# Four graph-attention layers on one core: layer 0's norms computed during layer 3, and layer 3's first head in whole chunks

## The chip, the cores and the metric

The kernel runs on one core of a Trainium2 chip. A core has a matrix engine (TensorE, PE in the profile, with its weight loads shown as PEld), a vector engine (VectorE, DVE), an activation engine (ScalarE, ACT), a general one (GpSimd, POOL) and a queue engine (SyncE, SP), with SBUF as working memory, PSUM as the memory that PE writes its products to, and DMA queues between SBUF and HBM. The metric is the device time of one execution in microseconds (us); lower is better. The kernel before takes 2933.27 us, the median of 3 runs (2932.54 to 2933.40).

## What is computed

16 graphs ("batches") of 1024 nodes with 256 features go through four layers of graph attention. The input x is 16x1024x256 in float32, and adj, of 0 and 1, is 16x1024x1024. Every layer begins with a norm and adds its attention to x:

```python
h = jnp.maximum(_layernorm(x, axis=-1), 0.0)
x = x + _Ll_gnn_ref(h, adj, W, a)          # l = 0, 1, 2, 3
```

Layer 0 shows the pattern. A weight between node i and node j is a function of one number per row plus one number per column, masked by adj, and the weights sum the projected nodes:

```python
Wh = jnp.einsum('bnf,fo->bno', h, W)
f1 = Wh @ a1
f2 = Wh @ a2
e = jax.nn.leaky_relu(f1[:, :, None] + f2[:, None, :], negative_slope=SLOPE)
e = jnp.where(adj == 0, NEG_INF, e)
attention = jax.nn.softmax(e, axis=-1)
h_prime = jnp.einsum('bij,bjo->bio', attention, Wh)
```

Layers 1 and 2 have other functions of the sum, and an elu over the result. Layer 3 has four heads of 64 features; each has its own projection and weights, and its result goes through a relu, gets h added, and is normed over the 64 features.

## The kernel before, in words

**Layout.** A batch's 1024 nodes are NI = 8 blocks of P = 128 nodes on the partitions; `x_b` holds x as 128 x 8 x 256. Blocks are normed and projected in four pairs.

**A layer's start.** `project` (L315) takes a pair: DVE subtracts the mean and cuts at zero (`centered`, L302, or L325 for batch 0), PE turns the blocks (L338), ACT copies them to `hT` (L340), PE multiplies by W (L345) into an accumulator in PSUM, and `evict` takes it to `V` (L413 to L417) with a scale `rstd`, the inverse root of the squared deviations. For this `center_by_sums` (L299) lets ACT square the block with its mean as bias and sum it (L309), and POOL raises two columns to the power of minus a half (L292, L293). The sums for the means come with the previous layer's last operation, but in layer 0 nothing is before, so DVE sums x (L517). Batch 0 takes its statistics from another instruction (L323).

**Attention.** Exponentials of sums are products, so a weight is a maximum or minimum over a row of numbers and a column, times the mask. `weigh` (L354) lets PE spread one number per node over a `row` in PSUM (one buffer of 128 x 1024; L374, or L574 for layer 3's heads after the first), and DVE makes eight blocks of weights from it (L367), with eight buffers for each of two streams. `attend` (L445) multiplies the blocks with V on PE (L461), one block of result at a time, and projects finished pairs for the next layer in between.

**Layer 3.** Each head has two accumulators: `acc`, for values (`add_values`, L596), and `total`, for the sums of weights (`add_totals`, L606); both are filled by 32-column products through `in_tiles` (L581, L586). Four blocks of weights are a chunk, two chunks a head. Heads 1 to 3 do totals and values of a chunk together, and have the row of the next head (R in the change's name) placed ahead of the first chunk. Head 0 does the values of both chunks, then head 1's row is made from `thirds_T` (L640, L645), and then come the totals of both chunks. After each head ACT copies the two accumulators (L663), and after each copy comes a step of `testing` (a sum over one block of adj, L175) and one of `coming` (loads of the batch after next); PE turns the copies (L670, L678), DVE divides (L681), and `center` (L538) and `rescale` (L558) norm the head on DVE, ACT and POOL.

**Order.** Two streams, of even and odd batches, are generators that yield estimated times; at L719 to L727 the stream that is behind by these estimates goes on. A scheduler then settles each engine's order from that program order; operations handed to `keep_in_program_order` keep theirs, and products under `high_priority` go first. Each accumulator name has two PSUM buffers for each stream. `load` (L128) is the generator `coming`: it narrows adj through a DRAM buffer by POOL's DMA queue, turns it into `mask` by four DMA transposes on SP's queue (L155), and fetches x (L124), one step at a time; `x_b` and `mask` have three buffers, `ex`, the exponentials of layer 3, two.

Of the kernel before, what the change touches and what calls it, by code (L numbers as in the profile page):

```python
# [32 lines left out]
F32 = mybir.dt.float32  # L33
BF = mybir.dt.bfloat16
# [7 lines left out]
P = 128  # L42
# [19 lines left out]
def short_path(ctx: ExitStack, tc: tile.TileContext, ins: dict, out: bass.AP, bad: bass.AP):  # L62
# [65 lines left out]
    def load(b: int):  # L128


        narrow = narrows[b % 2]
        rows = narrow.bitcast(U8)
        if b == 0:

            for h in range(NH):
                for t in range(2):
                    cast = nc.gpsimd.dma_start(
                        halves[h].bitcast(U8).rearrange("(c t q) j -> t c q j", t=2, q=P)[t],
                        adj[b].rearrange("(c q t) j -> t c q j", t=2, q=P)[t, :, :, ts(h, HALF)],
                    )  # L140
                    tc.keep_in_program_order(cast)
        else:
            for c in range(NI // 2):
                cast = nc.gpsimd.dma_start(
                    rows.rearrange("(c t q) j -> c q t j", t=2, q=P)[c],
                    adj[b, ts(c, 2 * P), :].rearrange("(q t) j -> q t j", t=2),
                )
                tc.keep_in_program_order(cast)
        if b < 2:
            fetch_nodes(b)  # L150
        yield

        mask = masks[b] = nodes.tile([P, NI // 2, N, 2], U8, name="mask")
        for c in range(NI // 2):
            turn = nc.sync.dma_start_transpose(  # L155
                mask[:, c].rearrange("p n t -> p (n t)").bitcast(BF),
                halves[c // NH][:, ts(c % NH, P)] if b == 0 else narrow[:, ts(c, P)],
            )
            tc.keep_in_program_order(turn)
            yield  # L160
        if b > 1:
            fetch_nodes(b)
            yield

    def test(b: int):
# [130 lines left out]
    def accumulator(b: int) -> bass.AP:  # L296
        return psum.tile([P, HALF], F32, name=f"acc{b % 2}")

    def center_by_sums(xb: bass.AP, minus_mean: bass.AP, pair: int, centered: bass.AP) -> bass.AP:  # L299

        for n in range(2):
            nc.vector.tensor_scalar(  # L302
                centered[:, n, :], xb[:, 2 * pair + n, :], minus_mean[:, n : n + 1], 0.0,
                op0=ALU.add, op1=ALU.max,
            )
        squared = small.tile([P, 2], F32, name="squared")
        for n in range(2):
            square = work.tile([P, D], BF, name="square", bufs=1)
            nc.scalar.activation(  # L309
                square, xb[:, 2 * pair + n, :], AF.Square, bias=minus_mean[:, n : n + 1],  # L310
                accum_out=squared[:, n : n + 1],
            )
        return inverse_root(squared, 2, D, LN_EPS)

    def project(b: int, l: int, xb: bass.AP, sums: bass.AP, pair: int, evict):  # L315


        centered = work.tile([P, 2, D], F32, name="centered", bufs=3)
        if sums is None:
            mv = small.tile([P, 2, nc.vector.BN_AGGR_DIM], F32, name="mv", bufs=2)  # L320
            for n in range(2):
                stats = small.tile([P, nc.vector.BN_STATS_DIM], F32, name="stats", bufs=1)
                nc.vector.bn_stats(stats, xb[:, 2 * pair + n, :])  # L323
                nc.vector.bn_aggr(mv[:, n, :], stats)
                nc.vector.tensor_scalar(  # L325
                    centered[:, n, :], xb[:, 2 * pair + n, :], mv[:, n, 0:1], 0.0,
                    op0=ALU.subtract, op1=ALU.max,
                )
            rstd = inverse_root(mv[:, :, 1], 2, D, LN_EPS, D)
        else:  # L330
            minus_mean = small.tile([P, 2], F32, name="minus_mean")
            nc.vector.tensor_scalar_mul(minus_mean, sums[:, ts(pair, 2)], -1.0 / D)  # L332
            rstd = center_by_sums(xb, minus_mean, pair, centered)
        yield 0.5
        turned = psum.tile([P, NK, 2 * P], F32, name="misc")
        for n in range(2):
            for k in range(NK):
                nc.tensor.transpose(turned[:, k, ts(n, P)], centered[:, n, ts(k, P)], ident)  # L338
        hT = wide.tile([P, NK, 2 * P], F32, name="hT", bufs=3)
        nc.scalar.mul(hT, turned, ROOT_D)  # L340
        yield 1.0
        for n in range(2):
            projected = accumulator(b)[:, : D + EXT[l]]
            for k in range(NK):
                nc.tensor.matmul(  # L345
                    projected, hT[:, k, ts(n, P)], W[l][:, k, :],
                    start=(k == 0), stop=(k == NK - 1),
                )
            evict(2 * pair + n, projected, rstd[:, n : n + 1])
        yield 2.5  # L350
# [48 lines left out]
        )  # L399

    def batch(b: int):
        xb = xs.pop(b)
        if b == 0:
            next(preparing)
        coming = load(b + 2) if b + 2 < B else iter(())
# [21 lines left out]
        def begin3():  # L427
            h3 = last["h3"] = single.tile([P, NI, D], F32, name="h3")
            V3 = nodes.tile([P, NI, H, E + 1], F32, name="V", bufs=4)
            ex = last["ex"] = small.tile([P, NI, 3 * H], F32, name="ex", bufs=2)  # L430

            def evict3(i: int, projected: bass.AP, rstd: bass.AP):
                nc.scalar.activation(ex[:, i, :], projected[:, D:], AF.Exp, scale=rstd)
                nc.scalar.mul(h3[:, i, :], projected[:, :D], rstd)
                q = ex[:, i, :H].unsqueeze(2)
                nc.gpsimd.tensor_mul(
                    V3[:, i, :, :E], h3[:, i, :].rearrange("p (h e) -> p h e", h=H),
                    q.to_broadcast([P, H, E]),
                )
                nc.gpsimd.tensor_copy(V3[:, i, :, E:], q)  # L440
                nc.gpsimd.tensor_add(xb[:, i, :], xb[:, i, :], beta)  # L441

            return V3, evict3
# [63 lines left out]
            add_elu(xb[:, i, :], acc, total)  # L507

        V, evict = begin(0)
        sums = small.tile([P, NI], F32, name="sums_of_x")  # L510

        def first(pair: int):
            if b == 0:

                yield from project(b, 0, xb, None, pair, evict)
                return
            nc.vector.tensor_reduce(sums[:, ts(pair, 2)], xb[:, ts(pair, 2), :], AX.X, ALU.add)  # L517
            yield from project(b, 0, xb, sums, pair, evict)

        pairs = [first(pair) for pair in range(NI // 2)]  # L520
        for n in range(NI // 2 + 2):
            for pair in range(max(n - 2, 0), min(n + 1, NI // 2)):
                yield from islice(pairs[pair], 1)
# [82 lines left out]
        def add_totals(h: int, j: int):  # L606
# [4 lines left out]
            ]  # L611
            in_tiles(parts, total, j == 2, j == NI - 4)

        behind = weigh3(0)
        yield from start(behind, b)

# [7 lines left out]
        for h in range(H):  # L624
# [1 line left out]

            acc = accumulator(b)
            total = accumulator(b)
            if h == 0:
                for first in range(0, NI, 4):  # L630
                    for _ in range(4):
                        next(behind)
                    pinned = []
                    for j in (first + 2, first):
                        add_values(h, j)
                    yield 3.6
                for _ in behind:
                    pass
                turned_thirds = psum.tile([3 * QUAD, P], BF, name="misc")
                made = nc.tensor.transpose(  # L640
                    turned_thirds, thirds.rearrange("p t i h -> p (t i h)"), ident_bf
                )
                tc.keep_in_program_order(made)
                thirds_T = small.tile([3 * QUAD, P], BF, name="thirds_T", bufs=1)
                nc.scalar.copy(thirds_T, turned_thirds)  # L645
            behind = weigh3(h + 1)
            yield from start(behind, b)

            for first in range(0, NI, 4):
                pinned = []  # L650
                for j in (first + 2, first):
                    add_totals(h, j)
                    if h > 0:
                        add_values(h, j)
                for _ in range(4):
                    next(behind, None)
                yield 1.8 if h == 0 else 5.4
            for _ in behind:
                pass
            copies = []  # L660
            for accT in (acc, total) if h == 0 else (total, acc):
# [4 lines left out]
            sums, totals = copies if h == 0 else copies[::-1]  # L666
            yield 0.5
            turned = psum.tile([P, NG, P], F32, name="misc")
            for i in range(NG):
# [28 lines left out]
        for _ in coming:  # L698
# [406 lines left out]
```

## Time and profile before

| | |
|---|---|
| time, median of 3 runs | 2933.27 us (2932.54 to 2933.40) |
| the profiled execution's own time | 2933.13 us |
| its span, first to last instruction | 2931.4 us |
| mean granted PE clock | 0.995 |
| one repetition (one batch done) in the middle | 178.5 us, of which PE is busy 174.5, DVE 133.4, ACT 68.2, POOL 61.6 |
| products of layers 0 to 2 (L461) | 6144 records, 1435.6 us of PE |
| products of layer 3 (L586) | 6144 records, 691.7 us of PE |
| weights (L367) | 896, 1102.7 us of DVE |
| ACT's squares for the norms (L309) | 504, 255.7 us and 96.5 us of reading the sums |

A line of the profile's groups gives the source line, the engine, the operation, its result and sources with their sizes, the count, the busy time and the mean duration of one, and the idle time of the engine just before with what ended it. Each float32 product of PE stands as two records. In windows each engine's busy time in a stretch is followed by its count of instructions; a line of the waits says who waited for whom, with the sum, the count and the longest; a line in order of time gives start, duration, engine, line and operation, and in brackets the idle time before.

### The profile page before, as it was taken

Reading aid. Unit: us, or ns where it says so; the run is one execution under the profiler, and the core shown is the slowest. Engines: PE = TensorE matmul, PEld = TensorE weight load, DVE = VectorE, ACT = ScalarE, POOL = GpSimd, SP = SyncE. Lnnn points to the kernel's source line nnn. Section 1 sums busy time; section 2 is a strip of 40 time slices with the busy share of each in tenths; the row PEclk is TensorE's granted clock in tenths of the full one; section 3 lists DMA queues with packets and bytes.
Section 4 is the critical chain, followed back from the end, with each engine's and each line's share of the span. In section 5 each row is a group of like instructions: output and inputs, shape, how many; then the busy total and the mean of one; then the engine's idle time right before and its main releaser. Section 6 shows DMA issues by size and latency. Waiting matters only on the chain.

```text
span 2931.4 us, 44756 instructions
## 1 busy us (share of the span) xinstructions
PE 2810.0 (96%) x16790; PEld 1961.9 (67%) x16790; DVE 2147.9 (73%) x4490; ACT 1088.2 (37%) x3010; POOL 981.3 (33%) x1533
## 2 busy tenths in 40 slices
PE   7999999999999999999999999999999999999986
PEld 5775857668576685766758577685766857667552
DVE  5658688586976859778586885868768587685857
ACT  1333434343343433424334343433434334343332
POOL 2123324243242423424233242432424224242333
PEclk9999999999999999999999999999999999999998
DMA  8204022030321303122031220303203031110101
GB/s 126 39 8 65 30 30 58 8 51 29 37 51 16 56 17 51 37 29 59 1 51 37 30 58 8 51 30 37 51 12 47 29 49 39 15 30 1 22 22 31
DMA packets 127967, 106.14 MB, mean 36 GB/s; under 512 B 79872, under 2 KB 98432, under 8 KB 127744
## 3 DMA queue, kind: packets, MB, share of 16 engines
q0 software_dynamic: 47328, 66.10, 15.4%
q1 hardware_dynamic: 79568, 35.53, 5.4%
q8 instruction: 135, 2.21, 0.3%
q10 hardware_dynamic: 848, 1.57, 0.2%
q14 instruction: 88, 0.72, 0.1%
HBM read 153.49 MB, written 33.55 MB: 64 GB/s over the span
## 4 chain that ended last, share of the span: by engine, by line
PE 59%; DVE 26%; issue 8%; POOL 3%; ACT 3%; DMA 0%; POOLq 0%; ACTq 0%; SPq 0%; DVEq 0%
PE acc L461 36%; DVE weights L367 16%; PE acc L586 10%; PE acc L345 9%; PE misc L338 2%; DVE centered L302 2%; POOL rstd L293 2%; DVE V L417 1%; PE row L374 1%; POOL y L544 1%; DVE y L545 1%; DVE var L555 1%; ACT square L309 1%; DVE y L551 1%; DVE mean L549 1%
## 5 line engine op out<-in xcount | busy, mean ns | idle before, releaser
L461 PE MATMUL acc<-V,weights 128*128 128x257 f32 x6144 | 1435.6, 384 | 33.5 <-DVE weights L367 15.7
L461 PEld LDWEIGHTS acc<-V,weights 128*128 128x128 f32 x6144 | 1136.6, 190 | 281.9 <-DVE weights L367 75.3
L586 PE MATMUL acc<-weights,V 128*32 128x512 f32 x6144 | 691.7, 596 | 12.0 <-DVE weights L367 8.1
L367 DVE SCALAR_TENSOR_TENSOR weights<-row,ex,mask 128x1024 f32<-128x1024 f32 x512 | 629.0, 1272 | 97.3 <-PE row L574 65.8
L345 PE MATMUL acc<-W,hT 128*128 128x259 f32 (+1 forms) x2048 | 516.1, 389 | 38.1 <-ACT hT L340 26.9
L367 DVE SCALAR_TENSOR_TENSOR weights<-row,V,mask 128x1024 f32<-128x1024 f32 x384 | 473.7, 1273 | 0.8 <-PE row L374 0.8
L345 PEld LDWEIGHTS acc<-W,hT 128*128 128x128 f32 x2048 | 378.7, 190 | 135.1 <-ACT hT L340 44.4
L586 PEld LDWEIGHTS acc<-weights,V 128*32 128x32 f32 x6144 | 189.1, 110 | 417.7 <-issue 410.3
L393 ACT ACTIVATE below<-acc,inv 128x256 f32<-128x256 f32 x256 | 121.1, 473 | 813.1 <-DVE inv L386 569.6
L293 POOL TENSOR_TENSOR rstd<-rstd,minus_half 128x2 f32<-128x2 f32 (+1 forms) x321 | 292.8, 912 | 20.3
L309 ACT ACTIVATE square<-x_b,minus_mean 128x256 bf16<-128x256 f32 x504 | 255.7, 507 | 110.3 <-DVE minus_mean L332 105.3
L441 POOL TENSOR_TENSOR x_b<-x_b,beta 128x256 f32<-128x256 f32 x128 | 93.5, 731 | 488.6 <-ACT square L309 483.5
L292 POOL TENSOR_SCALAR rstd<-squared 128x2 f32<-128x2 f32 x252 | 80.0, 317 | 464.0 <-ACT square L309 451.0
L385 DVE TENSOR_SCALAR inv<-acc 128x1 f32<-128x1 f32 x256 | 39.1, 153 | 255.3 <-PE acc L461 254.0
L302 DVE TENSOR_SCALAR centered<-x_b,minus_mean 128x256 f32<-128x256 f32 x504 | 195.7, 416 | 5.1
L340 ACT ACTIVATE hT<-misc 128x512 f32<-128x512 f32 x256 | 150.2, 592 | 129.6 <-PE misc L338 129.3
L396 DVE SCALAR_TENSOR_TENSOR x_b<-below,x_b 128x256 f32<-128x256 f32 x256 | 131.8, 515 | 84.9 <-ACT below L393 83.0
L663 ACT COPY sums<-acc 128x512 f32<-128x512 f32 x128 | 74.9, 585 | 308.6 <-PE acc L586 301.0
L413 ACT ACTIVATE V<-acc,rstd 128x3 f32<-128x3 f32 x384 | 98.4, 261 | 231.1 <-PE acc L345 230.6
L417 DVE TENSOR_SCALAR V<-acc,rstd,V 128x256 f32<-128x256 f32 x256 | 131.4, 537 | 59.8 <-ACT V L413 58.9
L338 PE MATMUL misc<-ident,centered 128*128 128x128 f32 x1024 | 158.7, 277 | 13.7 <-DVE centered L325 11.5
L170 POOL DMA_DIRECT2D adj_i<-in_adj_dram x128 | 74.4, 582 | 290.1 <-ACT adj_i L175 248.8
(96 smaller groups left out, 2212.8 us busy)
## 6 DMA issues: line engine op xcount, KB each, us to landing
adj_i<-in_adj_dram POOLq DMA_DIRECT2D x128, 256.0 KB, 3.9
x_b<-in_x_dram SPq DMA_DIRECT2D x15, 1024.0 KB, 6.4
narrow<-in_adj_dram POOLq DMA_DIRECT2D x60, 256.0 KB, 9.3
out_dram<-y POOLq DMA_DIRECT2D x30, 512.0 KB, 7.5
x_b<-in_x_dram ACTq DMA_DIRECT2D x4, 256.0 KB, 6.1
narrow_half<-in_adj_dram POOLq DMA_DIRECT2D x4, 256.0 KB, 16.9
mask<-narrow SPq DMA_TRANSPOSE x60, 3.7
weights<-in_L_gnn_a_dram SPq DMA_DIRECT2D x3, 256.0 KB, 5.5
```

The costliest lines, as they stand in the source:

```text
L293: nc.gpsimd.tensor_tensor(r, r, minus_half.to_broadcast([P, n]), op=ALU.pow)
L302: nc.vector.tensor_scalar(centered[:, n, :], xb[:, 2 * pair + n, :], minus_mean[:, n : n + 1], 0.0, op0=ALU.add, op1=ALU.max,)
L309: nc.scalar.activation(square, xb[:, 2 * pair + n, :], AF.Square, bias=minus_mean[:, n : n + 1], accum_out=squared[:, n : n + 1],)
L338: nc.tensor.transpose(turned[:, k, ts(n, P)], centered[:, n, ts(k, P)], ident)
L340: nc.scalar.mul(hT, turned, ROOT_D)
L345: nc.tensor.matmul(projected, hT[:, k, ts(n, P)], W[l][:, k, :], start=(k == 0), stop=(k == NK - 1),)
L367: nc.vector.scalar_tensor_tensor(w, r, c(j), masks[b][:, j // 2, :, j % 2], op0=op, op1=ALU.mult)
L393: nc.scalar.activation(below, acc[:, :D], AF.Exp, scale=inv)
L396: nc.vector.scalar_tensor_tensor(xi, below, 1.0, xi, op0=ALU.min, op1=ALU.add)
L417: nc.vector.tensor_scalar(V[:, i, :D], projected[:, :D], rstd, V[:, i, D : D + 1], op0=ALU.mult, op1=ALU.mult,)
L461: nc.tensor.matmul(accs[i], weights[j][:, ts(i, P)], V[:, j, : D + 1], start=(j == 0), stop=(j == NI - 1),)
L586: made = nc.tensor.matmul(accT[ts(n, QUAD), :], values, moving, start=first, stop=last)
```

## The change

1. `norm_ahead` computes the statistics of layer 0 of the batch after next while a batch's layer 3 goes on: ACT sums each block in an Identity pass, POOL makes the negative means, ACT squares and sums, and after the last pair POOL makes all eight `rstd` at once. It has eight steps, two after each head of layer 3 (`next(ahead, None)`). Batch 1's are made in one go at its start; batch 0 keeps its own. `project` takes them as a pair of tiles, so the DVE sums (L517) and the squares in layer 0 go.
2. `load` fetches x ahead of the mask's transposes, and takes its step once before layer 3's heads.
3. Head 0 of layer 3 does totals and values of a chunk together, and the source makes head 1's row, and four of its weights, ahead of head 0's second chunk.
4. `ex` has one buffer.

```diff
-        if b < 2:
-            fetch_nodes(b)
+        if b > 1:
+            yield
+        fetch_nodes(b)
         yield
...
-            yield
-        if b > 1:
-            fetch_nodes(b)
             yield
...
+    def norm_ahead(b: int):
+        totals = small.tile([P, NI], F32, name="totals_of_x", bufs=1)
+        minus_mean = small.tile([P, NI], F32, name="minus_means", bufs=2)
+        squared = small.tile([P, NI], F32, name="squares_of_x", bufs=1)
+        for pair in range(NI // 2):
+            for i in (2 * pair, 2 * pair + 1):
+                square = work.tile([P, D], BF, name="square", bufs=1)
+                tc.keep_in_program_order(
+                    nc.scalar.activation(
+                        square, xs[b][:, i, :], AF.Identity, accum_out=totals[:, i : i + 1]
+                    )
+                )
+            nc.gpsimd.tensor_scalar_mul(
+                minus_mean[:, ts(pair, 2)], totals[:, ts(pair, 2)], -1.0 / D
+            )
+            yield
+            for i in (2 * pair, 2 * pair + 1):
+                square = work.tile([P, D], BF, name="square", bufs=1)
+                tc.keep_in_program_order(
+                    nc.scalar.activation(
+                        square, xs[b][:, i, :], AF.Square, bias=minus_mean[:, i : i + 1],
+                        accum_out=squared[:, i : i + 1],
+                    )
+                )
+            yield
+        rstd = small.tile([P, NI], F32, name="first_rstd", bufs=2)
+        nc.gpsimd.tensor_scalar_add(rstd, squared, D * LN_EPS)
+        nc.gpsimd.tensor_tensor(rstd, rstd, minus_half.to_broadcast([P, NI]), op=ALU.pow)
+        norms_ahead[b] = minus_mean, rstd
...
+        elif isinstance(sums, tuple):
+            minus_mean, rstd = (a[:, ts(pair, 2)] for a in sums)
+            relu_centered(xb, minus_mean, pair, centered)
...
     def batch(b: int):
+        if b == 1:
+            for _ in norm_ahead(b):
+                pass
         xb = xs.pop(b)
+        ahead = norm_ahead(b + 2) if b + 2 < B else iter(())
...
-            nc.vector.tensor_reduce(sums[:, ts(pair, 2)], xb[:, ts(pair, 2), :], AX.X, ALU.add)
-            yield from project(b, 0, xb, sums, pair, evict)
...
+        next(coming, None)
         behind = weigh3(0)
         yield from start(behind, b)
...
-            if h == 0:
-                for first in range(0, NI, 4):
+            if h > 0:
+                behind = weigh3(h + 1)
+                yield from start(behind, b)
+
+            for first in range(0, NI, 4):
+                if h == 0:
                     for _ in range(4):
                         next(behind)
-                    pinned = []
-                    for j in (first + 2, first):
-                        add_values(h, j)
-                    yield 3.6
...
+                if h == 0 and first > 0:
+                    for _ in behind:
+                        pass
...
+                    behind = weigh3(1)
+                    yield from start(behind, b)
+                    for _ in range(4):
+                        next(behind)
                 pinned = []
                 for j in (first + 2, first):
                     add_totals(h, j)
-                    if h > 0:
-                        add_values(h, j)
-                for _ in range(4):
-                    next(behind, None)
-                yield 1.8 if h == 0 else 5.4
+                    add_values(h, j)
+                if h > 0 or first > 0:
+                    for _ in range(4):
+                        next(behind, None)
+                yield 5.4
...
                 next(testing)
                 next(coming, None)
+                next(ahead, None)
```

`relu_centered` is the loop at L301 to L305 as a function of its own.

More of the change, by code (lines that the diff above doesn't have):

```diff
@@ L297, in accumulator, with relu_centered @@
         return psum.tile([P, HALF], F32, name=f"acc{b % 2}")
-    def center_by_sums(xb: bass.AP, minus_mean: bass.AP, pair: int, centered: bass.AP) -> bass.AP:
+    def norm_ahead(b: int):
[27 more added lines that the diff above has]
+        norms_ahead[b] = minus_mean, rstd
+    norms_ahead = {}
+    def relu_centered(xb: bass.AP, minus_mean: bass.AP, pair: int, centered: bass.AP):
         for n in range(2):
@@ L305, in center_by_sums @@
             )
+    def center_by_sums(xb: bass.AP, minus_mean: bass.AP, pair: int, centered: bass.AP) -> bass.AP:
+        relu_centered(xb, minus_mean, pair, centered)
         squared = small.tile([P, 2], F32, name="squared")
@@ L329, in project @@
             rstd = inverse_root(mv[:, :, 1], 2, D, LN_EPS, D)
+        elif isinstance(sums, tuple):
+            minus_mean, rstd = (a[:, ts(pair, 2)] for a in sums)
+            relu_centered(xb, minus_mean, pair, centered)
         else:
@@ L429, in begin3 @@
             V3 = nodes.tile([P, NI, H, E + 1], F32, name="V", bufs=4)
-            ex = last["ex"] = small.tile([P, NI, 3 * H], F32, name="ex", bufs=2)
+            ex = last["ex"] = small.tile([P, NI, 3 * H], F32, name="ex", bufs=1)
             def evict3(i: int, projected: bass.AP, rstd: bass.AP):
@@ L509, in batch @@
         V, evict = begin(0)
[L510 to L516, printed above, removed]
-            nc.vector.tensor_reduce(sums[:, ts(pair, 2)], xb[:, ts(pair, 2), :], AX.X, ALU.add)
-            yield from project(b, 0, xb, sums, pair, evict)
-        pairs = [first(pair) for pair in range(NI // 2)]
+        known = None if b == 0 else norms_ahead.pop(b)
+        pairs = [project(b, 0, xb, known, pair, evict) for pair in range(NI // 2)]
         for n in range(NI // 2 + 2):
@@ L628, in batch @@
             total = accumulator(b)
-            if h == 0:
-                for first in range(0, NI, 4):
+            if h > 0:
[3 more added lines that the diff above has]
+                if h == 0:
                     for _ in range(4):
                         next(behind)
-                    pinned = []
-                    for j in (first + 2, first):
-                        add_values(h, j)
-                    yield 3.6
[L637 to L649, printed above, removed]
+                if h == 0 and first > 0:
+                    for _ in behind:
+                        pass
+                    turned_thirds = psum.tile([3 * QUAD, P], BF, name="misc")
+                    made = nc.tensor.transpose(
+                        turned_thirds, thirds.rearrange("p t i h -> p (t i h)"), ident_bf
+                    )
+                    tc.keep_in_program_order(made)
+                    thirds_T = small.tile([3 * QUAD, P], BF, name="thirds_T", bufs=1)
+                    nc.scalar.copy(thirds_T, turned_thirds)
+                    behind = weigh3(1)
+                    yield from start(behind, b)
+                    for _ in range(4):
+                        next(behind)
                 pinned = []
@@ L660, in batch @@
             copies = []
-            for accT in (acc, total) if h == 0 else (total, acc):
+            for accT in (total, acc):
                 copies.append(wide.tile([P, HALF], F32, name="sums"))
@@ L665, in batch @@
                 next(coming, None)
-            sums, totals = copies if h == 0 else copies[::-1]
+                next(ahead, None)
+            totals, sums = copies
             yield 0.5
@@ L697, in batch @@
             yield 1.0
-        for _ in coming:
+        for _ in chain(coming, ahead):
             pass
```

## The prediction

> **What bounds the kernel now.** I read the page first, then one repetition in windows, then the waits of TensorE (PE), then the order of time around layer 3's first head. The first line says where the limit is:
>
> ```profile
> PE 2810.0 (96%) x16790; PEld 1961.9 (67%) x16790; DVE 2147.9 (73%) x4490; ACT 1088.2 (37%) x3010; POOL 981.3 (33%) x1533
> ```
>
> PE leaves 121 us. Fourteen stretches of 178.5 us from 200 us on hold the same work and, but for the first, 174.3 to 174.5 us of busy PE: one batch is finished per 178.5 us, and PE idles 4.0 us in each. In windows of 5.1 us (1092 to 1260 us), PE is full but for a few rows:
>
> ```profile
> core 0: us, PE busy (x) PEld busy (x) DVE busy (x) ACT busy (x) POOL busy (x), PEclk, DMA share, GB/s
> 1107.50:1112.60 5.10, 5.10 (x40) 2.91 (x36) 5.10 (x6) 2.77 (x8) 1.17 (x2) 1.00 0.46 62
> ...
> 1122.80:1127.90 5.10, 4.85 (x24) 3.69 (x20) 5.10 (x7) 2.74 (x6) 1.82 (x4) 1.00 0.54 77
> 1127.90:1133.00 5.10, 4.14 (x21) 2.85 (x22) 4.59 (x9) 1.18 (x4) 5.08 (x6) 1.00 0.65 62
> ...
> 1189.10:1194.20 5.10, 3.43 (x22) 2.83 (x20) 4.86 (x11) 4.18 (x17) 3.94 (x6) 1.00 0.00 0
> 1194.20:1199.30 5.10, 4.72 (x22) 3.69 (x23) 4.25 (x7) 2.16 (x8) 4.86 (x5) 1.00 0.00 0
> ```
>
> The 1122 to 1133 rows are layer 3's head 1 of one batch beside a layer-1 product of the other; 1189 to 1199 is the start of the next batch's layer 0. The waits of PE in this repetition give the reasons:
>
> ```profile
> PE acc L345 <- ACT hT L340: 1.7, 1, 1.7
> PE acc L461 <- DVE weights L367: 0.6, 1, 0.6
> PE acc L461 <- ACT above L395: 0.5, 1, 0.5
> PE acc L345 <- DVE V L417: 0.4, 1, 0.4
> PE acc L586 <- DVE inverses L385: 0.3, 1, 0.3
> ```
>
> So 2.1 us of the 4.0 lie in layer 0, 1.4 in layer 3. Head 0 in order of time, PE, then VectorE (DVE), then ScalarE (ACT):
>
> ```profile
> 1100.49 5.36 PE L586 MATMUL acc<-weights,V 128*32 128x512 f32 x48
> 1105.78 0.62 PE L574 MATMUL row<-thirds_T,rows_of 96*128 96x128 bf16 x8
> 1106.24 0.61 PE L338 MATMUL misc<-ident,centered 128*128 128x128 f32 x4
> 1106.78 1.92 PE L586 MATMUL acc<-weights,V 128*32 128x512 f32 x16
> ...
> 1111.46 5.36 PE L586 MATMUL acc<-weights,V 128*32 128x512 f32 x48
> ```
>
> ```profile
> 1101.96 0.62 DVE L302 TENSOR_SCALAR centered<-x_b,minus_mean 128x256 f32<-128x256 f32 x2
> 1106.44 9.62 DVE L367 SCALAR_TENSOR_TENSOR weights<-row,ex,mask 128x1024 f32<-128x1024 f32 x8 [3.87 <-PE row L574]
> ```
>
> ```profile
> 1106.40 1.15 ACT L175 ACTIVATE adj_i<-adj_i,minus_half 128x1024 bf16<-128x1024 bf16 x1
> 1107.45 0.19 ACT L175 ACTIVATION_READ_ACCUMULATOR adj_i<-adj_i,minus_half 128x1 f32 x1
> 1107.54 0.58 ACT L340 ACTIVATE hT<-misc 128x512 f32<-128x512 f32 x1
> ```
>
> DVE waits 3.87 us for head 1's row (1105.78), then makes eight weights at 1.20 us each. PE meanwhile does the 16 records of totals left over from head 0 (1.85 us to the next start) and fill, and starts head 1 at 1111.46, which needs weight 3: ready at 1106.44 + 4 x 1.20 = 1111.25. It fits by 0.2 us.
>
> **What the Trainium skill says.** "PSUM — Partial Sum Buffer", section "Engine vs sequencer instructions": ACT, DVE and GpSimd (POOL) are strict first-in first-out, matmuls start and end in program order. The trace agrees (DVE idles 3.87 us at the row), so a walk along each queue is fair. "Perfetto Trace Analysis", "Tensor Engine Instruction (MATMUL, LD_WEIGHTS)": PE's ends are modelled. It shows: 20 L461 records at 1123.05 and 12 at 1128.25 take until 1131.60, 8.55 us, where 32 take 6.93 elsewhere (1244.03 to 1250.96): 1.6 us lost, 0.6 shown. The same page, "Matmuls": groups should rotate through PSUM banks so that eviction overlaps; here each stream has two accumulators, so a late eviction stops PE (above L395, 0.5 us). "ScalarE: Activation LUTs", "What ACT_TABLE_LOAD costs": 186 + 0.833 N ns with immediate operands, an estimate of 0.40 us at N = 256; the trace's nearest row, L309 with its accumulator read, goes 0.63 us start to start (1102.02, 1102.65). I use 0.63.
>
> **A, head 0 in whole chunks.** No instruction comes or goes. In the built order PE's second chunk of head 0 still stands ahead of head 1's row, though the source has the row first; the totals of both chunks are now ahead of it too. Chunk 1 starts as before, at 1095.79 (it needs weight 3 of head 0). Then chunk 5.29 (1100.49 to 1105.78) -> 1101.08, projection and thirds transpose 1.1 -> 1102.2, weight 7 is there at 1101.4, chunk 5.29 -> 1107.5, row: 1.7 later than 1105.78. Behind the row PE has transposes 0.54, totals' transposes 0.44, a projection 1.86, sums' transposes 0.53: 3.37 us where it had 5.22. DVE needs 0.2 + 4 x 1.20 = 5.0 as before: PE waits 1.65, and head 1 starts at 1113.1. (ACT's new passes hold hT back, so 0.96 of this shows at the projection and the rest at the chunk; the end is the same.) Is it given back? DVE is full from 1106.44 to 1131, in the same order, so its weights come 1.7 later and the waits at 1123 to 1133 stay. From 1132.7 to 1184 PE shows no idle and cannot catch up. A = +1.65. If a cover behind the row were kept it would be 0.
>
> **B, norms ahead on ACT.** Added per batch: 8 Identity passes x 0.63 = 5.0 us; moved from layer 0: 8 squares, 5.0 us. All 16 go into layer 3's heads, four per head. Queued behind them are the other stream's hT, below and above, and V, which PE waits for. ACT idles 36.8 us per repetition at below L393 <- DVE inv, so most are covered. Walking the queues with +1.65: (1) four passes (2.5 us) stand ahead of below, above and hT after head 1; hT comes at 1149.25, PE's projection is there at 1148.75: 0.5. (2) the accumulator behind it is freed 0.4 late by V's eviction, queued after two squares; (3) after head 2 the above pass comes two squares late, 1166.7 against 1166.3: 0.4. B = +1.3; bounds 0 (all covered) and 8 visits x 1.26 = 10.
>
> **POOL and DMA.** POOL loses 4 x (0.317 + 0.912) = 4.9 and gains 4 means (nearest row L292, 0.317) plus one sum and power over 8 columns (0.20 + 1.64): 3.1. It is 33% busy and each mean comes before ACT's next square: 0. The fetch of x goes ahead of the four mask transposes on SP; it starts at 1020.83, when x_b's third buffer is released, so it moves nothing; transposes of 983 go behind it to 1021, and are used only after 1205: 0. ex with one buffer: head 3's last use is at 1161.7, the next batch's first write at 1224.5: 60 us of room, 0.
>
> **C, layer 0.** DVE loses 4 x 0.671 of sums and 4 x 0.195 of means, 3.5 us. Three sums lie at 1145 to 1148, one at 1163, where PE sets the pace: worth nothing. In layer 0 DVE is near full, 1184 to 1206, and its order changes: the first weight (1193.10) stood ahead of y L560 and filled the 2.1 us that L560 waits for POOL's rstd; now y comes first and DVE idles about 1.6 us. Walk: last sums' transposes 1188.85, y 1190.4, POOL's bias 1192.0, mean to difference 1194.55, square on ACT, sum 1195.9, POOL to 1198.0, y 1198.65, weights 0 to 7 with two pairs of V until 1209.2. Before it was 1205.6, plus A and B and 0.2 of overheads 1208.75. PE no longer waits 1.7 for hT but 2.0 for weight 0. C = +0.4; bounds -2.85 (the 2.05 shown and 0.8 hidden in the L461 run at 1202.40 are freed) and +1.6.
>
> **Sum.** A for 15 batches with another behind: 24.8. B + C for the 14 with a batch two on: 14 x 1.7 = 23.8. Batch 1's 16 passes in a row at its start: 10 us on an ACT a third busy; 0 to 5, I take 1. Together 49.6 on 2933.13, the profiled execution's own time (span 2931.4, 1.7 around it; the median shown is 2933.27): 2983.
>
> **Rivals.** (1) A alone: ACT's passes fit its idle time, C is 0: 2933 + 25 = 2958. ACT's 37% speaks for it, the strict queue against. (2) Faster: layer 0 is freed, C = -2.85, with B at 0: per repetition 1.65 - 2.85 = -1.2, 2933 + 25 - 40 = 2918. For it: 2.1 of PE's 4.0 idle lie there, and ACT's squares stood ahead of hT. Against: DVE's near-full run. It decides once C frees more than 1.65 + B. (3) ACT in the way, B = 5, half its bound: 2933 + 25 + 14 x 5.4 = 3034. For it: two accumulators per stream. (4) A cancels C: 2933.
>
> **How the numbers follow.** Forecast 0.50, (1) 0.25, (2) 0.10, (3) 0.10, (4) 0.05. Within 0.2%, 5.9 us, a measurement here can't tell from no change. Faster is (2), 0.10; same is (4), 0.05; slower the rest, 0.85. The range leaves out (2), (4) and the far half of (3): 2942 to 3012, where C at its better bound and B at 1.3 just falls out and B at 3.3 still falls in.
>
> **What would show it.** A: DVE's wait at head 1's row grows from 3.9 to about 5 us, PE idles 1.6 us or more just before head 1's first chunk. B: PE waits for hT or above while ACT is in an Identity or Square pass of the next x. C: layer 0's wait for hT shrinks and one of about 2 us for weights appears. The repetition is 181.9 us. Wrong if it is under 179, if head 1's chunk starts without a wait, or if ACT's passes stop PE eight times a batch.

## The result, and the profile after

| | before | after |
|---|---|---|
| time, median of 5 runs | 2933.4 us (2932.54 to 2934.81) | 3008.01 us (3006.37 to 3008.51) |
| ratio | 1 | 1.0253, 95% interval 1.0238 to 1.0268 |
| span of the profiled execution | 2931.4 us | 3006.4 us |
| mean granted PE clock | 0.995 | 0.988 |
| PE idle in a repetition in the middle | 4.0 us | 7.2 us |

The changed kernel is 74.6 us slower; the forecast was 50 us slower. The page after gives these busy times, and this chain of work that ended last, as shares of the span by engine:

```profile
PE 2832.1 (94%) x16790; PEld 1975.8 (66%) x16790; DVE 2112.2 (70%) x4370; ACT 1147.5 (38%) x3250; POOL 942.2 (31%) x1503
...
PE 52%; DVE 27%; issue 8%; ACT 6%; POOL 5%; DMA 1%; POOLq 0%; ACTq 0%; DVEq 0%; SPq 0%
```

DVE has 35.7 us and POOL 39.1 us less to do than before, ACT 59.3 us more. The chain before was

```profile
PE 59%; DVE 26%; issue 8%; POOL 3%; ACT 3%; DMA 0%; POOLq 0%; ACTq 0%; SPq 0%; DVEq 0%
```

Work was taken off DVE and POOL, and yet more of the chain runs through them and less through PE. The longest waits of PE in one repetition (1123.58 to 1305.94 us), as sum, times and longest:

```profile
PE acc L503 <- DVE weights L405: 2.7, 2, 2.0
PE acc L383 <- ACT hT L378: 1.2, 2, 0.7
PE acc L620 <- DVE weights L405: 1.2, 1, 1.2
...
```

L383, L503 and L620 are the lines that were L345, L461 and L586. The 1.7 us for hT has become 0.7, and two waits for weights have come: 2.0 us in layer 0, 1.2 us in layer 3. Head 0 and the start of head 1 on PE, and then the row's weights on DVE:

```profile
1135.29 5.36 PE L620 MATMUL acc<-weights,V 128*32 128x512 f32 x48
1140.58 0.62 PE L608 MATMUL row<-thirds_T,rows_of 96*128 96x128 bf16 x8
...
1142.55 2.02 PE L383 MATMUL acc<-W,hT 128*128 128x259 f32 x8 [0.46 <-ACT hT L378]
...
1146.15 1.06 PE L620 MATMUL acc<-weights,V 128*32 128x512 f32 x8 [1.15 <-DVE weights L405]
```

```profile
1141.24 9.63 DVE L405 SCALAR_TENSOR_TENSOR weights<-row,ex,mask 128x1024 f32<-128x1024 f32 x8 [5.05 <-PE row L608]
```

The row is made at 1140.58, behind all of head 0's second chunk. DVE stands still for 5.05 us. PE has only transposes and a projection left to do, waits 0.46 us for ACT's hT and then 1.15 us for the weights that DVE makes from the row. The other stretch is the one in which the next batch's layer 0 is projected. It is called layer 0 here, as in the prediction, but the weights made in it are those of the other stream's layer 2; layer 0's own row comes only at 1248.75. DVE and then PE:

```profile
1231.37 0.69 DVE L594 TENSOR_TENSOR y<-y,rstd 128x512 f32<-128x512 f32 x1 [1.60 <-POOL rstd L291]
1231.98 3.66 DVE L405 SCALAR_TENSOR_TENSOR weights<-row,V,mask 128x1024 f32<-128x1024 f32 x3
```

```profile
1233.32 1.13 PE L503 MATMUL acc<-V,weights 128*128 128x257 f32 x4 [2.00 <-DVE weights L405]
```

The first weight stands behind y, y waits 1.60 us for POOL, and PE waits 2.00 us for the weight.

To place the 75 us of span, take the start of `rest` (before L618, after L653), which POOL makes once per batch at the head of layer 3. The first comes after the loads. Of the fifteen intervals the first fourteen are one batch each; the last one, and what follows it, have less work of another batch beside them. For all kernels of this study, in us of the profiled execution:

| | to the first `rest` | first interval | mean of the next 13 | last interval | after the last `rest` | span | median time |
|---|---|---|---|---|---|---|---|
| before | 196.5 | 180.0 | 178.53 | 150.9 | 83.2 | 2931.4 | 2933.4 |
| after | 201.6 | 191.7 | 182.55 | 153.3 | 86.6 | 3006.4 | 3008.0 |
| e1 head 0 in chunks alone | 198.6 | 181.2 | 180.30 | 152.6 | 87.6 | 2963.8 | 2965.2 |
| e2 after, old head 0 | 200.9 | 190.7 | 180.89 | 151.3 | 81.7 | 2976.2 | 2979.2 |
| e3 chunks, row first | 196.9 | 177.2 | 177.09 | 149.4 | 81.2 | 2906.8 | 2908.2 |
| e4 after, row first | 201.2 | 188.5 | 178.93 | 149.4 | 81.8 | 2946.9 | 2946.9 |
| e5 = e4, y put off | 201.6 | 188.4 | 176.26 | 150.0 | 80.9 | 2912.2 | 2912.7 |
| e6 = e4, batch 1's own norms | 196.6 | 188.8 | 178.81 | 149.4 | 81.7 | 2941.0 | 2942.8 |
| e7 = e4, adj one ahead | 200.8 | 179.3 | 178.70 | 149.9 | 80.6 | 2933.7 | 2936.7 |
| e8 = e4, no passes on ACT | 196.9 | 182.5 | 179.04 | 148.9 | 80.4 | 2936.2 | 2940.9 |
| e9 = e4 with e5, e6, e7 | 197.0 | 176.3 | 176.21 | 150.2 | 81.0 | 2895.2 | 2897.1 |
| e10 = e3, y put off | 196.3 | 175.8 | 175.53 | 149.4 | 82.0 | 2885.4 | 2887.1 |
| e11 after, no passes on ACT | 198.6 | 188.3 | 182.77 | 152.9 | 87.1 | 3002.9 | 3005.2 |
| e12 before, y put off | 197.0 | 178.8 | 177.00 | 151.4 | 81.5 | 2909.7 | 2912.3 |

The 75.0 us between before and after are 5.1 up to the first `rest`, 11.7 in the first interval, 13 x 4.02 = 52.3 in the steady state, 2.4 in the last interval and 3.5 at the end. The forecast had 3.4 per repetition, 1 at the start and nothing for the end.

### The profile page after: what moved, and what is told of

It reads as the page before. It is cut to its first block, busy times and chain, and to the rows that moved or that the text cites. A ratio compares the mean times of both kernels' runs of the same rounds, so it can differ in the third digit from the quotient of the medians.

```text
span 3006.4 us, 44693 instructions
## 1 busy us (share of the span) xinstructions
PE 2832.1 (94%) x16790; PEld 1975.8 (66%) x16790; DVE 2112.2 (70%) x4370; ACT 1147.5 (38%) x3250; POOL 942.2 (31%) x1503
## 3 DMA queue, kind: packets, MB, share of 16 engines
q0 software_dynamic: 47328, 66.10, 15.5%
## 4 chain that ended last, share of the span: by engine, by line
PE 52%; DVE 27%; issue 8%; ACT 6%; POOL 5%; DMA 1%; POOLq 0%; ACTq 0%; DVEq 0%; SPq 0%
PE acc L503 31%; DVE weights L405 18%; PE acc L620 10%; PE acc L383 9%; POOL y L578 2%; PE misc L376 2%; ACT square L343 2%; POOL rstd L291 2%; DVE y L579 1%; ACT below L431 1%; DVE x_b L435 1%; DVE x_b L434 1%; DVE var L589 1%; DVE y L585 1%; DVE mean L583 1%
## 5 line engine op out<-in xcount | busy, mean ns | idle before, releaser
L503 PE MATMUL acc<-V,weights 128*128 128x257 f32 x6144 | 1440.5, 386 | 61.3 <-DVE weights L405 43.5
L503 PEld LDWEIGHTS acc<-V,weights 128*128 128x128 f32 x6144 | 1142.1, 191 | 311.8 <-DVE weights L405 103.6
L620 PE MATMUL acc<-weights,V 128*32 128x512 f32 x6144 | 690.8, 598 | 31.2 <-DVE weights L405 27.3
L383 PE MATMUL acc<-W,hT 128*128 128x259 f32 (+1 forms) x2048 | 516.9, 392 | 36.1 <-ACT hT L378 21.5
L620 PEld LDWEIGHTS acc<-weights,V 128*32 128x32 f32 x6144 | 192.5, 110 | 449.1 <-issue 422.6
L383 PEld LDWEIGHTS acc<-W,hT 128*128 128x128 f32 x2048 | 381.4, 192 | 125.7 <-ACT hT L378 29.9
L343 ACT ACTIVATE square<-x_b,minus_mean 128x256 bf16<-128x256 f32 x384 | 195.2, 508 | 220.0 <-DVE minus_mean L370 210.0
L291 POOL TENSOR_TENSOR rstd<-rstd,minus_half 128x2 f32<-128x2 f32 (+2 forms) x261 | 248.6, 952 | 16.3
L378 ACT ACTIVATE hT<-misc 128x512 f32<-128x512 f32 x256 | 151.0, 596 | 189.1 <-PE misc L376 188.8
L290 POOL TENSOR_SCALAR rstd<-squared 128x2 f32<-128x2 f32 x192 | 37.5, 195 | 477.0 <-ACT square L343 467.5
L376 PEld LDWEIGHTS misc<-ident,centered 128*128 128x128 f32 x1024 | 122.7, 144 | 61.6 <-issue 18.8
L173 ACT ACTIVATE adj_i<-adj_i,minus_half 128x1024 bf16<-128x1024 bf16 x128 | 147.3, 1151 | 15.5 <-DMA adj_i<-in_adj_dram 15.5
L435 DVE SCALAR_TENSOR_TENSOR x_b<-above,x_b 128x256 f32<-128x256 f32 x256 | 122.1, 477 | 18.6 <-ACT hT L378 0.9
```

Of the source, the lines that this page charges most:

```text
L173: square = nc.scalar.activation(adj_i, adj_i, AF.Square, bias=minus_half, accum_out=squares[:, b, i : i + 1])
L291: nc.gpsimd.tensor_tensor(r, r, minus_half.to_broadcast([P, n]), op=ALU.pow)
L343: nc.scalar.activation(square, xb[:, 2 * pair + n, :], AF.Square, bias=minus_mean[:, n : n + 1], accum_out=squared[:, n : n + 1],)
L383: nc.tensor.matmul(projected, hT[:, k, ts(n, P)], W[l][:, k, :], start=(k == 0), stop=(k == NK - 1),)
L435: nc.vector.scalar_tensor_tensor(xi, above, 0.0, xi, op0=ALU.add, op1=ALU.add, accum_out=total)
L503: nc.tensor.matmul(accs[i], weights[j][:, ts(i, P)], V[:, j, : D + 1], start=(j == 0), stop=(j == NI - 1),)
```

## The experiments

**Head 0 and the norms apart (e1, e2).** e1 is the kernel before with the new loop over head 0. e2 is the changed kernel with the old loop: it has the norms ahead, and with them the earlier fetch of x and the single `ex`.

```diff
 # e1, against before            # e2, against after: the reverse
-            if h == 0:
-                for first in range(0, NI, 4):
...
-                        add_values(h, j)
-                    yield 3.6
...
                 for j in (first + 2, first):
                     add_totals(h, j)
-                    if h > 0:
-                        add_values(h, j)
+                    add_values(h, j)
```

> The kernel before with layer 3's head 0 in whole chunks and nothing else. Theory (the sum of the prediction, A a third to a half of the steady loss): PE waits about 1.6 us more before head 1's first chunk, once per batch; repetition 178.5 + 1.65 = 180.2 us, time 2933 + 25 = 2958 us, with the clock and the start as before. Rival 1 (the whole loss comes from head 0, the norms are free): about 3008 us. Rival 2 (the norms carry it all): about 2933 us.

> The changed kernel with head 0 as before: values of both chunks first, then the totals. Theory: what A doesn't explain stays, 4.0 - 1.65 = 2.4 us per repetition times 13, 31 us, and the longer start and end, 17 and 6 us: about 2985 us (2970 to 2990). Rival 1 (head 0 is the whole loss): about 2933 us. Rival 2 (the norms carry it all): about 3008 us.

e1 took 2965.2 us (ratio to the kernel before 1.0107, 95% interval 1.0090 to 1.0124), e2 2979.2 us (1.0155, 1.0138 to 1.0172). That is 31.5 and 45.5 us more, together 77 for the 74.6 of the whole change. The two halves add up and both lose, so both rivals fall. In e1 the same place on PE reads

```profile
1117.65 0.62 PE L574 MATMUL row<-thirds_T,rows_of 96*128 96x128 bf16 x8
...
1120.05 2.02 PE L345 MATMUL acc<-W,hT 128*128 128x259 f32 x8 [0.90 <-ACT hT L340]
...
1123.22 1.06 PE L586 MATMUL acc<-weights,V 128*32 128x512 f32 x8 [0.71 <-DVE weights L367]
```

DVE's wait at the row is 5.05 us here too. 0.90 + 0.71 = 1.61 us of waits, and 180.30 - 178.53 = 1.77 us per repetition. What e1 adds at the end, 4.4 us after the last `rest`, is not in the prediction: there no other stream gives PE work while DVE makes the weights. Before head 1's first chunk PE idles 4.16 us in e1 where it idled 1.37 us before. e1, and then before:

```profile
2900.34 7.05 PE L586 MATMUL acc<-weights,V 128*32 128x512 f32 x48 [4.16 <-DVE weights L367]
```

```profile
2870.56 5.36 PE L586 MATMUL acc<-weights,V 128*32 128x512 f32 x48 [1.37 <-DVE weights L367]
```

**Where the row stands (e3, e4).** The source of the change has head 1's row ahead of head 0's second chunk, the built order has it behind. The first product of a chunk isn't held behind anything (`pinned` is empty), and the others follow it with high priority. Holding it back is enough:

```diff
-                pinned = []
+                pinned = [0] if h == 0 and first > 0 else []
```

> Head 0 in whole chunks, with the first product of its second chunk held behind head 1's row, so that PE makes the row ahead of the second chunk. Theory (head 1 is late because its row is made behind the second chunk): DVE's wait at the row falls from about 5 to under 2 us, PE doesn't wait before head 1's chunk, and the time is 2933 us or up to 20 us less. Rival (the loss of whole chunks is not the row's place but the totals now ahead of it, and so the same work in another order): as with whole chunks alone, about 2958 us.

> The changed kernel with the same hold, so that head 1's row stands ahead of head 0's second chunk on PE. Theory: A's loss goes and the rest stays, 3008 - 25 = 2983 us (2970 to 2990), repetition about 180.5 us. Rival (the row's place isn't what costs): 3008 us.

e3 took 2908.2 us (0.9913, 0.9897 to 0.9930), e4 2946.9 us (1.0044, 1.0027 to 1.0061). This is more than either expectation had. The row's place is worth 57.0 us to head 0 in chunks and 61.2 us to the changed kernel, nearly twice what A cost (31.5). It doesn't only undo the loss, it turns it round. e3, PE and then DVE:

```profile
1094.44 0.61 PE L574 MATMUL row<-thirds_T,rows_of 96*128 96x128 bf16 x8
1094.98 5.36 PE L586 MATMUL acc<-weights,V 128*32 128x512 f32 x48
```

```profile
1095.09 9.62 DVE L367 SCALAR_TENSOR_TENSOR weights<-row,ex,mask 128x1024 f32<-128x1024 f32 x8 [0.27 <-PE row L574]
```

DVE waits 0.27 us instead of 5.05, head 1's chunk starts without a wait, and PE's 0.6 us for weights in the layer-1 product behind head 1, there in the kernel before too, is gone. The repetition is 177.09 us, 1.44 less than before.

**Layer 0: weights behind y (e5, e10, e12).** e5 puts off the last head's rescale (L594) and the output's DMAs to the next layer 0 of the stream, behind that layer's own first weight, and so behind all eight weights of the other stream; e10 does the same to e3, which has no norms ahead, and e12 to the kernel before.

```diff
-        while normed:
-            rescale(*normed.pop(0), ...)
-        for g in range(NH):
-            ...
+        def complete(pin=False): ...      # those lines; DVE's multiply kept in program order
+        if b + 2 < B:
+            held[b + 2] = lambda: complete(True)
+        else:
+            complete()
...
                 next(behind)
+                if l == 0 and j == 0 and b in held:
+                    held.pop(b)()
                 product(0, j)
```

> e4 with the last head's rescale and the output's DMAs put off to the next layer 0 of the stream, behind its first weight, so that DVE makes the weights without first waiting for POOL's rstd. Theory (C: PE's 2.0 us at layer 0's first weight is DVE's 1.6 us at rstd plus y): that wait of PE goes, hT or V late next, 1 to 2 us less per repetition, 177.0 to 177.8 us, time 2922 to 2935 us. Rival (the weights are late for another reason, such as the row): as e4, 2947 us.

> e3 (head 0 in chunks, row first, no norms ahead) with the last head's rescale and output put off as in e5. Theory (the put-off only undoes the order that the norms ahead brought; without them weight 0 stands ahead of y already and PE waits there for hT, behind ACT's squares): as e3, repetition 176.8 to 177.1 us, time 2904 to 2909 us, so the norms ahead are worth about 0.9 us per repetition once their order is mended. Rival (the put-off itself frees DVE and is worth it anywhere): repetition 176.1 us or less, time under 2895 us, and the norms ahead are worth nothing.

> The kernel before with nothing but the put-off of e5 and e10. Theory (what e10 gained over e3, 21 us, comes from layer 0 alone and doesn't depend on head 0): repetition 177.0 us, time about 2912 us. Rival (in the kernel before, layer 0 has hT as its last wait, and the put-off is worth something only beside the row's new place): repetition 178.0 to 178.5 us, time 2926 to 2934 us.

e5 took 2912.7 us (0.9926, 0.9910 to 0.9943), 34.2 us less than e4. Its repetition on PE has no wait for weights left:

```profile
PE acc L384 <- ACT hT L379: 0.7, 1, 0.7
PE acc L384 <- ACT above L434: 0.5, 2, 0.3
PE acc L504 <- ACT above L434: 0.5, 1, 0.5
PE acc L625 <- DVE inverses L424: 0.3, 1, 0.3
```

So the weights were late for y and nothing else. e10 and e12 show that this is not a matter of the norms ahead alone: e10 took 2887.1 us (0.9838, 0.9822 to 0.9854), 21.1 us less than e3, and e12 2912.3 us (0.9927, 0.9910 to 0.9944), 21.4 us less than before. The theory in e10's expectation was wrong and its rival right; the theory in e12's was right. The put-off is worth 1.53 us per repetition with neither part of the change in place. DVE sets the pace of this stretch with the other stream's eight weights. y among them costs it 0.84 us of waiting for rstd and 0.69 us of work, together 1.53. In e12, y stands behind layer 0's own first weight and waits for nothing. Before, and then e12:

```profile
1195.22 0.69 DVE L560 TENSOR_TENSOR y<-y,rstd 128x512 f32<-128x512 f32 x1 [0.84 <-POOL rstd L293]
```

```profile
1206.56 0.69 DVE L564 TENSOR_TENSOR y<-y,rstd 128x512 f32<-128x512 f32 x1
```

PE's waits show little of this gain: the one of 1.7 us for hT stays in e12. In e4, y costs 1.60 + 0.69 = 2.3 us, and e5 gains 2.67, more than expected; a lower PE clock behind e4's wait (last section) comes to about the rest.

**ACT's passes (e8, e11).** Both leave out ACT's two passes of the norms ahead, e8 from e4, e11 from the changed kernel.

```diff
-            for i in (2 * pair, 2 * pair + 1):
-                square = ...
-                    nc.scalar.activation(square, xs[b][:, i, :], AF.Identity, accum_out=...)
...                                                    # and the same for AF.Square
-        totals = small.tile([P, NI], F32, name="totals_of_x", bufs=1)
+        totals = squared = fixed          # a constant
```

> e4 with ACT's Identity and Square passes of the norms ahead left out; POOL takes its sums from a constant, so layer 0's statistics are not those of x. Theory (B is ACT's passes in the way of hT, above and V in layer 3): 0.9 to 1.3 us less per repetition, and C stays with PE's 2.0 us at the first weight: repetition 177.5 to 177.9 us, and with the start's 10 to 15 us back, time about 2920 us. Rival (passes are covered, C is all of the norms' loss): repetition as e4, 178.8 us, time 2932 to 2937 us by the start alone.

> The changed kernel with ACT's Identity and Square passes of the norms ahead left out; POOL takes its sums from a constant, so layer 0's statistics are not those of x. Theory by e8 (the passes are covered in the steady state, B is 0): repetition as the changed kernel, 182.3 to 182.7 us; with about 10 us less at the start, time 2996 to 3000 us. Rival (B as predicted, 1.3 us: in the changed kernel's own order hT and above are later than in e4's): repetition about 181.2 us, time about 2980 us.

The repetition is 179.04 us in e8 against 178.93 in e4 (178.81 and 178.70 in e6 and e7 below), and 182.77 in e11 against 182.55 after. ACT has 7.5 us less to do in each, and nothing comes of it. For the repetition the theory of e8 falls, and its rival and the theory of e11 hold. e8 took 2940.9 us and e11 3005.2 us, 4 and 5 us above what these two expected. What the passes do cost lies at the start: e8 is 6.0 us faster than e4 in the median, and its profiled execution is 4.3 us ahead at the first `rest` and gains 5.9 more in the first interval. One repetition of e8:

```profile
PE acc L489 <- DVE weights L391: 2.3, 2, 2.0
PE acc L369 <- ACT hT L364: 0.7, 1, 0.7
PE acc L489 <- ACT above L419: 0.5, 1, 0.5
...
```

The waits for hT and above, which looked like ACT's passes in the way, are there without the passes. In the changed kernel itself PE waits 0.52 us for hT after head 1, which on ACT stands behind `below`, and `below` behind four passes. After, PE, ACT and DVE:

```profile
1181.94 0.66 PE L715 MATMUL misc<-ident,sums 128*128 128x128 f32 x4 [0.52 <-ACT hT L378]
```

```profile
1179.94 0.51 ACT L317 ACTIVATE square<-x_b,minus_means 128x256 bf16<-128x256 f32 x1
...
1180.56 0.48 ACT L431 ACTIVATE below<-acc,inv 128x256 f32<-128x256 f32 x1
```

```profile
1180.30 0.16 DVE L424 RECIPROCAL inv<-inv 128x1 f32<-128x1 f32 x1
```

e11, without the passes:

```profile
1176.78 0.66 PE L701 MATMUL misc<-ident,sums 128*128 128x128 f32 x4 [0.50 <-ACT hT L364]
```

```profile
1175.40 0.48 ACT L417 ACTIVATE below<-acc,inv 128x256 f32<-128x256 f32 x1 [2.67 <-DVE inv L410]
```

Where the passes were, ACT idles in e11 until DVE's `inv` comes. With the passes `inv` comes no earlier: it ends at 1180.46, just as the passes do. Counted from `rest`, `below` starts at 56.98 us after and at 56.96 in e11. The passes only fill a gap.

What the norms ahead do cost in layer 3 goes with another order of PE's products. Behind the row, e3 does the next chunk at once; e4 first does transposes, a projection and 16 records of the other stream. Counted from `rest`, the whole chunks of layer 3 start alike in e3, e4 and e8 up to 47.85 us; then e3 has them at 54.6, 62.2 and 81.8, e4 at 60.5, 73.1 and 82.5 and e8 at 60.6, 73.1 and 82.5. From there on e4 and e8 are 0.7 us behind. In the changed kernel the same loss is larger: its last chunk starts at 86.35 us, that of e11 at 86.31 and that of e1 at 85.00. Why the scheduler chose that order was not tried.

**The start (e6, e7).** e6 lets batch 1 make its norms as before; e7 fetches each of batch 0's blocks of adj one block earlier.

```diff
 # e6
-        if b == 1:
-            for _ in norm_ahead(b):
-                pass
...                                                    # batch 1's sums on DVE, as before
 # e7, in test
+            if b > 0 or i == 0:
+                fetch(i)
+            if b == 0 and i + 1 < NI:
+                fetch(i + 1)
```

> e4 with batch 1's norms made as in the kernel before (DVE's sums, squares in its own layer 0), all others ahead. Theory (batch 1's 16 passes in a row hold up ACT at the start): the first rest comes at 197 instead of 201.2 us, the first repetition stays at about 188, time 2943 us. Rival 1 (they are also the cause of the slow first repetition): 2932 us. Rival 2 (the passes are hidden, something else holds the start up): 2947 us.

> e4 with batch 0's blocks of adj fetched one block earlier than they are squared. Theory (in batch 0 these fetches are held in program order on POOL, behind the new means, which wait for ACT behind the square of the block fetched last, so that each of ACT's squares waits out a whole fetch): ACT's waits for adj_i in the first repetition fall from 1 to 4 us each to under 1, PE's clock stays up, and the first repetition goes from 188.5 to 178 to 181 us: time 2937 to 2940 us. Rival (the first repetition is long for the passes of the norms themselves): 2947 us.

e6 took 2942.8 us (1.0030, 1.0019 to 1.0042): the first `rest` comes 4.5 us earlier, at 196.6, and the first interval stays at 188.8. e7 took 2936.7 us (1.0010, 1.0002 to 1.0019): the first interval falls from 188.5 to 179.3. Each mends its own place, as the theories had it. What e7 took away is seen on POOL and ACT in the kernel after:

```profile
272.43 0.60 POOL L168 DMA_DIRECT2D adj_i<-in_adj_dram  x1
...
279.11 0.22 POOL L310 TENSOR_SCALAR minus_means<-totals_of_x 128x2 f32<-128x2 f32 x1 [4.06 <-ACT square L306]
279.32 0.61 POOL L168 DMA_DIRECT2D adj_i<-in_adj_dram  x1
```

```profile
276.37 1.15 ACT L173 ACTIVATE adj_i<-adj_i,minus_half 128x1024 bf16<-128x1024 bf16 x1 [4.01 <-DMA adj_i<-in_adj_dram]
...
277.51 0.58 ACT L378 ACTIVATE hT<-misc 128x512 f32<-128x512 f32 x1
277.99 0.40 ACT L306 ACTIVATE square<-x_b 128x256 bf16<-128x256 f32 x1
```

In batch 0 alone the fetches of adj keep their program order (L169). The one at 279.32 stands behind the mean at 279.11, the mean waits for ACT's pass at 277.99, and that stands behind the square at 276.37, which waits for the fetch issued at 272.43. So each fetch is issued only when the last has been used, and hT at 277.51 waits too. ACT's waits for adj in this stretch (200 to 395 us) sum to 8.1 us before, 15.5 after, 18.4 in e4 and 2.3 in e7. PE is busy for only 6.6 of 10 us here, and its granted clock falls in the 10 us behind. Two windows of after, and then one of e7, give the length, the busy time of PE, of its weight loads, of DVE, ACT and POOL with their counts, the granted PE clock, the DMA share and GB/s:

```profile
270.00:280.00 10.00, 6.62 (x36) 5.47 (x35) 5.45 (x9) 5.65 (x17) 4.20 (x8) 0.96 0.18 26
280.00:290.00 10.00, 9.11 (x52) 3.63 (x56) 8.64 (x19) 5.80 (x17) 5.95 (x8) 0.69 0.17 28
```

```profile
280.00:290.00 10.00, 10.00 (x73) 5.45 (x72) 2.88 (x6) 4.21 (x11) 4.84 (x4) 1.00 0.37 69
```

**All of it mended (e9).** The edits of e5, e6 and e7 together on e4.

> e4 with the edits of e5, e6 and e7 together: row first, weights before y, batch 1's own norms, adj one block ahead in batch 0. Theory (each mends its own place: 4.1 us up to the first rest, 9.2 us in the first repetition, 2.6 us per repetition): e5's 2912.7 less 4.1 less 10.2, about 2899 us, repetition 176.1 us. Rival (the longer start only gives back slack that later stages use up): about 2912 us, as e5.

e9 took 2897.1 us (0.9874, 0.9857 to 0.9890), as the theory had it. With its order mended in these four places, the change is 37 us faster than the kernel before. But e10, which has the chunks, the row first and y put off but no norms ahead, is 10 us faster still, at 2887.1 us and 175.53 us per repetition against 176.21. The norms ahead, with the earlier fetch of x and the single `ex`, cost 0.7 us per repetition even so. e10 is the best kernel of the study, 47 us below the one before.

## Why the prediction was right, and where it was wrong

The direction and head 0's mechanism were right. The time lies 25 us above the forecast and 4 us inside the upper end of the range: 8.7 us of the miss lie in the steady state (4.02 per repetition for 3.35), 12.4 at the start and in the first interval, and some 4 at the end. Part of being right was luck, as B shows. Step by step:

- **A, 1.65 per repetition: right.** Measured alone 1.77. The row behind the second chunk, DVE's wait of 5.0 (5.05) and PE's waits of 1.65 in two parts (0.46 and 1.15 after, 0.90 and 0.71 in e1) came as worked out. That ACT's new passes hold hT back there is not borne out: without them, in e1, PE's wait for hT is the longer one. The sum's "A for 15 batches with another behind" left out the last batch, where e1 loses 4.4 us after the last `rest` and the whole change 3.5.
- **B, 1.3 for ACT's passes: the size came, the cause was wrong.** e8 and e11 leave the passes out and the repetition stays. Two of the walk's three waits came where it had them, 0.5 for hT after head 1 (0.52) and 0.4 for above after head 2 (0.34), but e11 has them too, at 0.50 and 0.25. The passes do stand ahead there, and what sets the time is DVE's `inv`. What the norms ahead cost in layer 3 is 1.35 us in the changed kernel (86.35 against 85.00) and 0.7 in e4; it goes with PE's order, which no step had. That 1.3 was met is luck.
- **C, 0.4: the mechanism right, the size too small.** The wait of 2.0 us for weight 0 came to the tenth, but 0.7 of the wait for hT stays beside it. From DVE's last read of x's sums ahead of layer 0 to PE's last projection in it, layer 0 takes 0.73 us longer in e4 than in e3 (22.69 against 21.96), and as much longer after than in e1 (22.71 against 21.96). In six of thirteen repetitions of e4, and in five after, a lower PE clock adds 0.7, on average 0.3. With layer 3's 0.7 that makes about 1.8 for e4, which exceeds e3 by 1.84; with layer 3's 1.35 it makes 2.4 for the changed kernel, which exceeds e1 by 2.25, and for e2, which exceeds the kernel before by 2.36. The prediction had B + C = 1.7.
- **POOL at 0: wrong at the start.** The step compared busy times and ACT's next square. It did not ask what stands behind the new mean on POOL, and the fetches of adj of batch 0 do: 9.2 us of the first interval (e7, which takes away the waits of the kernel before too).
- **The start, 1 of at most 5:** 4.5 for batch 1's passes (e6) is near the upper bound. Of the first interval's 11.7 the sum had only the 3.4 of any repetition.
- **ex, and the fetch of x ahead of the transposes, at 0:** neither was tried alone. Every run with the norms ahead has both, so their share in what the norms ahead cost, and in PE's new order, stays open.
- **Rivals.** A alone was 2958 and measured 2965, but it isn't what the whole change does. Layer 0 freed needed C below nothing; y ahead of the weights decided against it. ACT in the way fell with B. A cancelling C fell with C above nothing. No rival had what makes the best kernels: that head 0 in chunks gains if the row really stands first. The step "If a cover behind the row were kept it would be 0" stopped one question short: with the row early, DVE's wait of 3.87 us in the kernel before nearly goes too (0.27), and the repetition is 1.44 us shorter.

## What to carry to other kernels

Price what a change does to the order, not only what its instructions take. Here 7.5 us of ACT passes per batch cost nothing in the steady state, while one product free to move ahead of a row, and one multiply among the weights, were worth 3.2 and 1.5 us per batch. For each new instruction that waits, list what stands behind it on its own queue, in the first and the last round too, where less of another stream covers it. A wait behind a new instruction is not yet a wait for it: ask when the work behind it would have been released without it. And when the source places work somewhere, see that the built order does: one missing hold turned a gain of 25 us into a loss of 31.

## What the runs showed of the hardware

The granted PE clock fell after short stalls. "TensorE: Matmul & The Clock Gate", section "Why this matters for your kernels", of the Trainium skill advises against idle gaps of PE above some 3 us, which drop the clock. Here less was enough at times: e4's layer 0 has the same two waits, 0.68 and 2.00 us with a projection between, in every repetition, and in six of thirteen the products after them are slow. What decides between the two was not found.

```profile
1385.45 2.02 PE L383 MATMUL acc<-W,hT 128*128 128x259 f32 x8 [0.68 <-ACT hT L378]
1389.47 1.13 PE L503 MATMUL acc<-V,weights 128*128 128x257 f32 x4 [2.00 <-DVE weights L405]
...
1390.77 1.77 PE L503 MATMUL acc<-V,weights 128*128 128x257 f32 x4
```

One repetition earlier the record that answers to the last line (1212.30) took 1.03 us. The clock over 30 us there (1373.6 to 1403.6) was 0.94, and 1.00 around it, and the repetition is 0.7 us longer. So these 2.7 us of waits cost at times a quarter as much again as the trace puts down for them.

ACT's 120 Identity passes with their sums took 0.40 to 0.45 us, in the median 0.42, and the read of the sum 0.19, with 0.53 us from one start to the next (after, 261.89 and 262.42). The 0.40 us that the prediction worked out from "ScalarE: Activation LUTs", section "What ACT_TABLE_LOAD costs", of the Trainium skill as an estimate is right for the pass; the 0.63 taken from the squares was too high.
